# A third Strassen-Winograd step for three more quarter products, with VectorE's sums around the gates in another order

## The chip, the cores and the metric

The kernel runs on one core of one Trainium2 chip. The metric is the device time of one execution in microseconds, the median of several runs. Smaller is better.

## The reference, cut to what matters

`x` is 8 batches of 256 tokens of 1024 features, all in f32. Two layers with a residual follow each other. The first is a dense layer with a routed low-rank update: the router's logits get a bias for the batch's language id, the two best of 8 experts are softmax-weighted, and rank 4 factors `A` and `B` of these experts are added. The second is a dense layer whose 1024 x 1024 weight is picked for each batch by its adapter id.

```python
base   = einsum('btd,od->bto', x, W)
logits = einsum('btd,ed->bte', x, Wr) + one_hot(language_ids, 8)[:, None, :] * 5.0
topw, topi = top_k(logits, 2)
gates  = sum(one_hot(topi, 8) * softmax(topw)[..., None], axis=-2)
h      = einsum('btd,erd->bter', x, A)
x = x + base + 2.0 * einsum('bter,bte,eor->bto', h, gates, B)
x = x + einsum('bsi,boi->bso', x, weight[adapter_ids])
```

## The kernel before, in words

Features and tokens are split in two, so `x`, `W` and the result `y` are 2 x 2 blocks of 512 features by 1024 tokens (`xb`, `wb`, `yb`, in the on-chip memory all along). The residual is an identity added to the diagonal of the weights (`add_identity`). The first layer multiplies the blocks by the Strassen-Winograd scheme: seven products instead of eight, in the order 1, 5, 2, 6, 3, 7, 4, with sums of blocks ahead (`w_sum`, `x_sum`, in pieces of 1024 elements a partition) and sums of results behind (`join`). Each of the seven does the same once more inside: blocks are split in quarters, seven quarter products are made of sums `s1`..`s3` of weights and `t1`..`t3` of x, and `late` turns `s2` and `t2` into the fourth sums when the second quarter product has read them. A quarter product (`mm`) is four matmuls of 128 x 128 weights by 512 columns into a pair of accumulator banks. An f32 matmul is two instructions on TensorE.

In products 5, 2, 3 and 4 the quarter a(0,1) x b(1,0) goes a third step down: seven matmuls of 256 columns (`deep`, L513) instead of four of 512, with sums r1..r4 and q1..q4 of 128 and 256 elements. Three of the seven, P2 to P4, go straight into the accumulator X; P1, P6 and P7 are added up in one bank (`A3`) which is read between them, and P5 has its own (`B3`). Product 1 (`opening`), 6 and 7 have no third step. There are eight banks: three pairs (`pair0` to `pair2`), which play the roles A, X and B in turn (`roles`), and two single ones.

The router and low-rank part is `project(j, c)`: for half j of the tokens and half c of that, 32 matmuls of 136 columns that give h and the logits, chunk k of the features after chunk k. `take` adds the bias on VectorE and copies h on ScalarE. `gating(j)` is 18 small VectorE instructions, one exponential on ScalarE and a product of 1024 elements; `turn(j)` transposes the gated h on TensorE, whence `hg`, whose matmuls with `b_sb` and its differences (`bdiff`, made by `b_differences`) join the quarter products ("lora").

The order on each engine is the order of the code. Ahead of product 5 it is written out at the end of the code: project(1, 0), take, project(1, 1), take, gating(1) on VectorE beside project(0, 1) on TensorE, turn(1), product 5. x is replaced by a difference in place there (`t1(c, k)`, eight pieces of 512 elements).

From product 5 on, VectorE's work for later products stands in a list `todo` with a time and an earliest place for each item. `pump(place)` is called at seven places of each product and takes items in order until their time reaches an even share of what is left; place 7 takes all. The list before product 5 holds gating(0), the w_sum of w11 (two pieces, which product 6 needs) and make_subs("2"); before product 2 it holds x_sum of x12, w_sum of w21, make_subs("6") and two pieces of an x sum.

The second layer (`adapt`, L660) is one such scheme of seven products for each batch; the last batch is cut finer at the end (`adapt_last`, L718). Its weights come by `load_w1` on SP's queue, block by block, when the blocks whose place they take have been read.

Of the kernel before, what the change touches and what calls it, by code (L numbers as in the profile page):

```python
# [9 lines left out]
F32 = mybir.dt.float32  # L10
# [15 lines left out]
def kernel(  # L26
# [320 lines left out]
    def us(n):  # L347
        return (n + 151) / 960
# [13 lines left out]
        return pieces(fn, wb[out_], wb[x], wb[y], 2)  # L362

    subs = {}

    def make_subs(key, w, x, further=True):

        def a(i, j):  # L370
            return wb[w][:, 2 * j : 2 * j + 2, i * OQ : (i + 1) * OQ]

        def b(i, j):
            return xb[x][:, 2 * i : 2 * i + 2, j * TQ : (j + 1) * TQ]


        ra = lambda i, j: a(0, 1)[:, j, ts(i, P)]
        rb = lambda i, j: b(1, 0)[:, i, ts(j, TQ // 2)]
        t = {}

        def op3(name, tag, fn, x, y, first=4):
            width = P if name[0] == "r" else TQ // 2

            def run():
                t[name] = sub3.tile([P, width], F32, name=f"{name}_{key}", tag=tag)
                fn(t[name], *(t[v] if isinstance(v, str) else v for v in (x, y)))

            return us(width), first, run

        deep = [  # L390
            op3("r1", "r13", add, ra(1, 0), ra(1, 1)),
            op3("q1", "q13", minus, rb(0, 1), rb(0, 0)),
            op3("r2", "r2", minus, "r1", ra(0, 0)),
            op3("q2", "q2", minus, rb(1, 1), "q1"),
            op3("r4", "r4", minus, ra(0, 1), "r2"),
            op3("q4", "q4", minus, rb(1, 0), "q2"),
        ]

        def deep3():
            for o in (  # L400
                op3("r3", "r13", minus, ra(0, 0), ra(1, 0)),
                op3("q3", "q13", minus, rb(1, 1), rb(0, 1)),
            ):
                o[2]()

        def op(name, fn, x, y, first):
            pool = sub2 if name[1] == "2" else sub1
            width = OQ if name[0] == "s" else TQ

            def run():  # L410
                t[name] = pool.tile([P, 2, width], F32, name=f"{name}_{key}", tag=name)
                fn(t[name], *(t[v] if isinstance(v, str) else v for v in (x, y)))

            return us(2 * width), first, run

        def late_s():
            minus(t["s2"], a(0, 1), t["s2"])

        def late_t():
            minus(t["t2"], b(1, 0), t["t2"])  # L420

        subs[key] = (a, b, t, (late_s, late_t), (ra, rb, deep3), further)
        return [
            op("s1", add, a(1, 0), a(1, 1), 3),
            op("t1", minus, b(0, 1), b(0, 0), 3),
            op("s2", minus, "s1", a(0, 0), 3),
            op("t2", minus, b(1, 1), "t1", 3),
            op("s3", minus, a(0, 0), a(1, 0), 5),
            op("t3", minus, b(1, 1), b(0, 1), 5),
        ] + (deep if further else [])  # L430

    def evict(dest, acc, base=None):

        if base is None:
            nc.scalar.copy(dest, acc)  # L435
        else:
            add(dest, acc, base)
# [20 lines left out]
    def opening(key, dest):  # L458


        idle = pair("idle", 2)
        for i in range(WARM):
            nc.tensor.matmul(idle[:, 0, :P], lhsT=ident, rhs=ident, start=True, stop=True)  # L463
        mm = multiply()
        sums_of = make_subs(key, "11", "11", False)
        a, b, t, late, _, _ = subs.pop(key)
        X = pair(f"X_{key}", 0)
        A = pair(f"A_{key}", 1)
        add_identity(wb["11"], 0, 2)
        mm(X, a(0, 1), b(1, 0), True, part=(0,))  # L470
        project(0, 0, singles("ps_h_0_0"), (2,), last=False)
        mm(X, a(0, 1), b(1, 0), part=(1,))
        evict(dest[:, 0], X)
        project(0, 0, None, (3,), False, False)
        mm(A, a(0, 0), b(0, 0), True, part=(0,))
        project(0, 0, None, (0,), False, False)
        mm(A, a(0, 0), b(0, 0), part=(1,))
        project(0, 0, None, (1,), False, False)
        use_adapter_ids()
        add_identity(wb["11"], 2, 4)  # L480
        for s in sums_of[:4]:
            s[2]()
        add(dest[:, 0], A, dest[:, 0])
        nc.tensor.matmul(idle[:, 1, :NB], lhsT=ones, rhs=ids_f[:, :NB], start=True, stop=True)
        use_ids(idle[:, 1, :NB])
        B = pair(f"B_{key}", 2)
        mm(B, t["s1"], t["t1"], True)
        evict(dest[:, 3], B)
        for s in sums_of[4:]:
            s[2]()  # L490
        mm(A, t["s2"], t["t2"])
        evict(dest[:, 1], A)
        project(0, 0, None, range(KH, KC), False)
        take(0, 0)
        for f in late:
            f()
        mm(A, t["s3"], t["t3"])
        add(dest[:, 3], A, dest[:, 3])
        mm(B, t["s2"], b(1, 1))
        add(dest[:, 1], B, dest[:, 1])  # L500
        mm(A, a(1, 1), t["t2"])
        evict(dest[:, 2], A)

    def product(key, base, dest, lora=None, tokens=None):

        a, b, t, late, (ra, rb, deep3), further = subs.pop(key)
        mm = multiply(dict(zip("01d", b_part(lora))) if lora is not None else None, tokens)
        new = roles(key)
        old = [base[:, q] if base is not None else None for q in range(4)]
        n0, n1 = (slice(j * (TQ // 2), (j + 1) * (TQ // 2)) for j in range(2))  # L510

        def deep(acc, lhs, rhs, first=False):
            nc.tensor.matmul(acc, lhsT=lhs, rhs=rhs, start=first, stop=True, skip_group_check=True)  # L513

        def quarter(m, n):

            return dest[:, 0][:, m, n], old[0][:, m, n] if base is not None else None

        A = new("A")
        mm(A, a(0, 0), b(0, 0), True)  # L520
        X = new("X")
        nc.scalar.copy(X, A)
        if not further:
            pump(1)
            B = new("B")
            mm(B, t["s1"], t["t1"], True, "1", 1)
# [17 lines left out]
            evict(dest[:, 2], A, old[2])  # L544
            pump(7)
            return
        A3 = single(f"A3_{key}", 0)[:, n0]
        deep(A3, ra(0, 0), rb(0, 0), True)
        q, o = quarter(0, n0)
        evict(q, A3, o)  # L550
        pump(1)
        B = new("B")
        mm(B, t["s1"], t["t1"], True, "1", 1, ms=(0,))
        B3 = single(f"B3_{key}", 1)[:, n0]
        deep(B3, t["r1"], t["q1"], True)
        deep3()
        mm(A, t["s2"], t["t2"])
        evict(dest[:, 1], A, old[1])
        deep(A3, t["r2"], t["q2"])
        q, o = quarter(0, n1)  # L560
        evict(q, A3, o)
        late[0]()
        pump(2)
        mm(B, t["s1"], t["t1"], True, "1", 1, ms=(1,))
        evict(dest[:, 3], B, old[3])
        late[1]()
        pump(3)
        deep(X[:, 0, n0], ra(0, 1), rb(1, 0))
        deep(X[:, 0, n1], t["r4"], rb(1, 1))
        deep(X[:, 1, n0], ra(1, 1), t["q4"])  # L570
        mm(X, None, None, False, "0", 0, part=())
        deep(A3, t["r3"], t["q3"])
        two = [P, 2, TQ // 2]
        d1 = dest[:, 0][:, 1, :].rearrange("p (j n) -> p j n", j=2)
        both = A3.unsqueeze(1).to_broadcast(two)
        evict(d1, both, old[0][:, 1, :].rearrange("p (j n) -> p j n", j=2) if base is not None else None)
        add(dest[:, 0][:, :, n1], B3.unsqueeze(1).to_broadcast(two), dest[:, 0][:, :, n1])
        add(dest[:, 0], X, dest[:, 0])
        pump(4)
        mm(A, t["s3"], t["t3"])  # L580
        add(dest[:, 3], A, dest[:, 3])
        pump(5)
        mm(B, t["s2"], b(1, 1), False, "d", 1)
        add(dest[:, 1], B, dest[:, 1])
        pump(6)
        mm(A, a(1, 1), t["t2"], False, "1", 0)
        evict(dest[:, 2], A, old[2])
        pump(7)
# [169 lines left out]


    opening("1", y21)  # L760
    b_differences()
    add_identity(wb["22"])
    for t in w_sum(add, "21", "21", "22"):
        t[2]()
    subs5 = make_subs("5", "21", "12")
    subs5[0][2]()
    subs5[2][2]()
    project(1, 0, halves(pair("ps_h_1_0", 0)))
    take(1, 0)

    def t1(c, k):
        minus(xk(k, 1, c), xk(k, 1, c), xk(k, 0, c))

    for k in range(KH):
        t1(0, k)
    project(1, 1, halves(pair("ps_h_1_1", 2)))
    take(1, 1)
    for t in gating(1):
        t[2]()
    for k in range(KH):  # L780
        t1(1, k)
    project(0, 1, singles("ps_h_0_1"))
    turn(1, halves(pair("ps_g_1", 2)))
    take(0, 1)
    for i in (1, 6, 7, 3, 8, 9, 10, 11, 4, 5):
        subs5[i][2]()
    todo += gating(0)
    todo += w_sum(minus, "11", "21", "11")
    todo += make_subs("2", "12", "21")
    product("5", None, y22, 1, 1)  # L790
    turn(0, singles("ps_g_0"))
    todo += x_sum(minus, "12", "22", "12")
    todo += w_sum(minus, "21", "22", "11")
    todo += make_subs("6", "11", "12", False)
# [79 lines left out]
```

## Time and profile before

| what | us |
|---|---|
| median of 3 runs (429.12 to 429.49) | 429.25 |
| the profiled execution, with what lies around its span | 430.16 |
| span of the profiled execution | 428.4 |
| TensorE busy (PE) | 423.1 |
| VectorE busy (DVE) | 281.7 |
| ScalarE busy (ACT) | 39.6 |

Instructions are named by engine, line, tile written and tiles read. PE is the matmul side of TensorE, PEld its weight loads. A time in brackets with an arrow is the idle time of the engine just before the instruction, and what ended it. Matmuls are pipelined: a duration reaches into the next one, so that the pace is read from the distance of starts.

### The profile page before, as it was taken

What the parts mean: (1) busy time and instruction counts of PE and PEld (TensorE: products, weight loads), DVE (VectorE), ACT (ScalarE), POOL (GpSimd) and SP (SyncE); (2) the same over time, 40 slices, a digit from 0 to 9 for tenths busy, and PEclk for the clock granted to TensorE, in tenths of its full rate; (3) what the DMA queues carried; (4) which work ended last, traced back from release to release, by engine and by line L of the source; (5) the groups of instructions that cost most, each with busy time, mean ns of one, the idle gap of its engine ahead of it and who ended that gap; (6) DMA issues with size and microseconds to landing.
All of it is one profiled execution on the core that took longest, in us unless ns stands there. A gap on an engine that the chain in (4) does not pass through costs nothing.

```text
span 428.4 us, 3335 instructions
## 1 busy us (share of the span) xinstructions
PE 423.1 (99%) x1246; PEld 217.3 (51%) x1246; DVE 281.7 (66%) x375; ACT 39.6 (9%) x65; POOL 2.0 (0%) x10
## 2 busy tenths in 40 slices
PE   8999999999999999999999999999999999999996
PEld 5566984545444445444454444444444444444574
DVE  1627288956988959889595676565756576565531
ACT  1120022110000000000000101010110101010110
POOL 1000000000000000000000000000000000000000
PEclk9999999999999999999999999999999999999999
DMA  8995000000000140630302276556748385550202
GB/s 279 383 398 217 2 0 2 0 0 2 0 0 0 31 168 0 249 142 0 99 0 98 98 262 227 199 207 208 272 148 313 128 275 214 196 197 0 98 2 99
DMA packets 14305, 55.83 MB, mean 130 GB/s; under 512 B 1232, under 2 KB 3536, under 8 KB 9808
## 3 DMA queue, kind: packets, MB, share of 16 engines
q1 hardware_dynamic: 12976, 54.68, 35.5%
q10 hardware_dynamic: 1248, 0.93, 0.7%
q8 instruction: 10, 0.16, 0.2%
q14 instruction: 7, 0.06, 0.0%
q0 software_dynamic: 64, 0.00, 0.0%
HBM read 47.22 MB, written 8.39 MB: 130 GB/s over the span
## 4 chain that ended last, share of the span: by engine, by line
PE 98%; DVE 0%; POOL 0%; issue 0%; ACT 0%; POOLq 0%; DVEq 0%
PE A L447 24%; PE A L660 22%; PE B L447 14%; PE B L660 13%; PE ps_h L245 7%; PE X L660 6%; PE X L447 4%; PE A_last L718 3%; PE A L513 1%; PE X L513 1%; PE idle L463 1%; PE ps_g L315 0%; PE B L513 0%; DVE y L217 0%; ACT z L748 0%
## 5 line engine op out<-in xcount | busy, mean ns | idle before, releaser
L660 PE MATMUL B<-x,x 128*128 128x512 f32 x128 | 57.5, 592 | 0.0
L447 PE MATMUL A<-t,s 128*128 128x512 f32 x112 | 50.3, 592 | 0.0
L217 DVE TENSOR_TENSOR y<-A,y 128x1024 f32<-128x1024 f32 (+2 forms) x27 | 26.3, 985 | 25.1 <-PE A L447 14.2
L660 PE MATMUL A<-w,x 128*128 128x512 f32 x88 | 39.6, 592 | 0.0
L660 PEld LDWEIGHTS B<-x,x 128*128 128x128 f32 x128 | 24.3, 190 | 29.8 <-issue 29.7
L217 DVE TENSOR_TENSOR w<-w,w 128x1024 f32<-128x1024 f32 x24 | 29.0, 1223 | 15.4 <-PE A L660 15.3
L660 PE MATMUL A<-w,y 128*128 128x512 f32 x88 | 39.1, 592 | 0.0
L447 PEld LDWEIGHTS A<-t,s 128*128 128x128 f32 x112 | 21.2, 190 | 22.9 <-issue 22.5
L245 PEld LDWEIGHTS ps_h<-y,x 128*128 128x128 f32 x256 | 30.7, 191 | 3.3 <-issue 3.3
L245 PE MATMUL ps_h<-y,x 128*128 128x136 f32 x256 | 30.6, 279 | 0.0
L660 PEld LDWEIGHTS A<-w,x 128*128 128x128 f32 x88 | 16.7, 190 | 21.0 <-issue 21.0
L660 PEld LDWEIGHTS A<-w,y 128*128 128x128 f32 x88 | 16.7, 190 | 21.0 <-issue 21.0
L435 ACT COPY z<-A 128x512 f32<-128x512 f32 x21 | 12.3, 586 | 158.3 <-PE A L660 158.3
L447 PE MATMUL B<-t,s 128*128 128x512 f32 x56 | 25.9, 594 | 0.3 <-DVE bias L200 0.3
L447 PE MATMUL A<-x,w 128*128 128x512 f32 x56 | 25.3, 592 | 0.0
L447 PE MATMUL A<-t,w 128*128 128x512 f32 x56 | 25.2, 592 | 0.0
L447 PE MATMUL B<-x,s 128*128 128x512 f32 x56 | 25.2, 592 | 0.0
L217 DVE TENSOR_TENSOR y<-B,y 128x1024 f32<-128x1024 f32 (+1 forms) x16 | 17.4, 1090 | 9.5 <-PE B L447 8.7
L217 DVE TENSOR_TENSOR x<-x,x 128x1024 f32<-128x1024 f32 (+1 forms) x20 | 19.2, 1004 | 0.0
L447 PEld LDWEIGHTS B<-x,s 128*128 128x128 f32 x56 | 10.6, 190 | 13.4 <-issue 12.7
L447 PEld LDWEIGHTS A<-t,w 128*128 128x128 f32 x56 | 10.6, 190 | 13.4 <-issue 12.7
L217 DVE TENSOR_TENSOR z<-X,z 128x512 f32<-128x512 f32 x8 | 5.5, 692 | 17.9 <-PE X L660 15.9
(119 smaller groups left out, 446.3 us busy)
## 6 DMA issues: line engine op xcount, KB each, us to landing
x<-w_dram SPq DMA_DIRECT2D x24, 1024.0 KB, 4.8
w<-w_dram SPq DMA_DIRECT2D x8, 1024.0 KB, 4.8
out_dram<-z SPq DMA_DIRECT2D x15, 512.0 KB, 3.0
x<-xT_dram SPq DMA_DIRECT2D x6, 1024.0 KB, 12.9
w<-wT_dram SPq DMA_DIRECT2D x3, 1024.0 KB, 14.9
x<-xT_dram SPq DMA_DIRECT2D x4, 256.0 KB, 3.8
x<-xT_dram SPq DMA_DIRECT2D x2, 512.0 KB, 7.4
w<-w11T_dram SPq DMA_DIRECT2D x1, 512.0 KB, 6.1
```

Source lines behind the costliest of these rows:

```text
L217: nc.vector.tensor_tensor(out_, x, y, op)
L245: nc.tensor.matmul(ps[v][:, u * EA : (u + 1) * EA], lhsT=xk(k, j, c)[:, ts(r, P)], rhs=aw_sb[:, k, :], start=(first and k == some[0] and u ...
L435: nc.scalar.copy(dest, acc)
L447: nc.tensor.matmul(acc[:, m, :], lhsT=l, rhs=r, start=(first and i < len(ms)), stop=(i >= len(steps) - len(ms)), skip_group_check=True,)
L463: nc.tensor.matmul(idle[:, 0, :P], lhsT=ident, rhs=ident, start=True, stop=True)
L513: nc.tensor.matmul(acc, lhsT=lhs, rhs=rhs, start=first, stop=True, skip_group_check=True)
L660: nc.tensor.matmul(accs[name], lhsT=lhs[:, k // 2, k % 2, :], rhs=rhs[:, k, :], start=(first and k == 0), stop=(k == KH - 1), skip_group_c ...
L718: nc.tensor.matmul(acc, lhsT=lhs[:, k // 2, k % 2, :], rhs=rhs[:, k, ts(v, m)], start=(first and k == 0), stop=(k == KH - 1), skip_group_c ...
```

## The change

A function `third` makes the sums and pieces of a third step for any quarter product: `ops` are r1 to q4, `ops3` r3 and q3, `piece(n)` is the matmul Pn, and `take(n, ...)` adds or copies the accumulated bank into the part of the result that it belongs to. Three more quarters use it: in product 1 the quarters with s2 x b(1,1) and a(1,1) x t2 (P3 and P4 of the quarter products), and in product 4 the one with a(1,1) x t2 (P4).

In product 1 the eight chunks of project(1, 0) are moved between the pieces, and b_differences with them. VectorE's x sums (now `x_t1`), s1 and s2 of product 5 are put in the order of their use: two x sums ahead of the gates, the other six and s1, s2 behind them. The ids' product goes into pair 0. The w_sum of w11 is put on the list after product 5, ahead of product 2's work.

```diff
+    def third(key, lhs, rhs):
...
+        ops = [
+            op("r1", "r13", add, A(1, 0), A(1, 1)),
+            op("q1", "q13", minus, B(0, 1), B(0, 0)),
+            op("r2", "r2", minus, "r1", A(0, 0)),
+            op("q2", "q2", minus, B(1, 1), "q1"),
+            op("r4", "r4", minus, A(0, 1), "r2"),
+            op("q4", "q4", minus, B(1, 0), "q2"),
+        ]
+        def ops3():
+            op("r3", "r13", minus, A(0, 0), A(1, 0))[2]()
+            op("q3", "q13", minus, B(1, 1), B(0, 1))[2]()
+        def piece(n, acc=None):
+            if n in (1, 5):
+                own[n] = single(f"P{n}_{key}", n // 5)[:, n0]
+            out_, l, r = {
+                1: lambda: (own[1], ra(0, 0), rb(0, 0)),
+                2: lambda: (acc[:, 0, n0], ra(0, 1), rb(1, 0)),
+                3: lambda: (acc[:, 0, n1], t["r4"], rb(1, 1)),
+                4: lambda: (acc[:, 1, n0], ra(1, 1), t["q4"]),
+                5: lambda: (own[5], t["r1"], t["q1"]),
+                6: lambda: (own[1], t["r2"], t["q2"]),
+                7: lambda: (own[1], t["r3"], t["q3"]),
+            }[n]()
+            nc.tensor.matmul(out_, lhsT=l, rhs=r, start=(n in (1, 5)), stop=True, skip_group_check=True)
...
 # opening
-        nc.tensor.matmul(idle[:, 1, :NB], lhsT=ones, rhs=ids_f[:, :NB], start=True, stop=True)
-        use_ids(idle[:, 1, :NB])
+        wide = pair("ids_wide", 0)[:, 0, :NB]
+        nc.tensor.matmul(wide, lhsT=ones, rhs=ids_f[:, :NB], start=True, stop=True)
+        use_ids(wide)
...
-        for f in late:
-            f()
+        late[0]()
+        ops, ops3, piece, out = third(f"{key}b", lambda: t["s2"], lambda: b(1, 1))
+        for o in ops:
+            o[2]()
+        late[1]()
         mm(A, t["s3"], t["t3"])
         add(dest[:, 3], A, dest[:, 3])
-        mm(B, t["s2"], b(1, 1))
+        quarter = halves(pair("ps_h_1_0", 0))
+        chunk = lambda k: project(1, 0, quarter, (k,), k == 0, k == KC - 1)
+        chunk(0)
+        piece(1)
+        out(1, dest[:, 1], dest[:, 1])
+        piece(5)
+        ops3()
+        chunk(1)
+        piece(6)
+        out(6, dest[:, 1], dest[:, 1])
+        chunk(2)
+        b_differences()
+        for n in (2, 3, 4):
+            piece(n, B)
+        chunk(3)
+        piece(7)
+        out(7, dest[:, 1], dest[:, 1])
+        last_out = out
+        ops, ops3, piece, out = third(f"{key}a", lambda: a(1, 1), lambda: t["t2"])
+        for o in ops[:2]:
+            o[2]()
+        last_out(5, dest[:, 1], dest[:, 1])
+        for o in ops[2:]:
+            o[2]()
         add(dest[:, 1], B, dest[:, 1])
-        mm(A, a(1, 1), t["t2"])
-        evict(dest[:, 2], A)
+        chunk(4)
+        piece(1)
+        out(1, dest[:, 2])
+        chunk(5)
+        piece(5)
+        ops3()
+        chunk(6)
+        piece(6)
+        out(6, dest[:, 2])
+        for n in (2, 3, 4):
+            piece(n, A)
+        chunk(7)
+        piece(7)
+        out(7, dest[:, 2])
+        out(5, dest[:, 2], dest[:, 2])
+        add(dest[:, 2], A, dest[:, 2])
...
 # product, for key 4 (two): after P5 of the first third step
+        if two:
+            ops, ops3, piece, take = third(f"{key}b", lambda: a(1, 1), lambda: t["t2"])
+            for o in ops:
+                o[2]()
...
         add(dest[:, 3], A, dest[:, 3])
+        if two:
+            piece(1)
+            take(1, dest[:, 2], old[2])
         pump(5)
         mm(B, t["s2"], b(1, 1), False, "d", 1)
+        if two:
+            piece(5)
+            ops3()
+            piece(6)
+            take(6, dest[:, 2], old[2])
         add(dest[:, 1], B, dest[:, 1])
         pump(6)
+        if two:
+            mm(A, None, None, False, "1", 0, part=())
+            for n in (2, 3, 4):
+                piece(n, A)
+            piece(7)
+            take(7, dest[:, 2], old[2])
+            take(5, dest[:, 2], dest[:, 2])
+            add(dest[:, 2], A, dest[:, 2])
+            pump(7)
+            return
...
 # around the gates
     opening("1", y21)
-    b_differences()
     add_identity(wb["22"])
     for t in w_sum(add, "21", "21", "22"):
         t[2]()
...
     take(1, 0)
+    x_t1(0, 0)
+    x_t1(0, 1)
     project(1, 1, halves(pair("ps_h_1_1", 2)))
     take(1, 1)
+    run(*(g[2] for g in gating(1)))
     project(0, 1, singles("ps_h_0_1"))
     turn(1, halves(pair("ps_g_1", 2)))
+    x_t1(1, 0)
+    x_t1(1, 1)
+    s1()
+    t1()
     take(0, 1)
+    x_t1(0, 2)
+    x_t1(0, 3)
+    run(r1, q1, s2)
+    x_t1(1, 2)
+    x_t1(1, 3)
+    run(t2, r2, q2, r4, q4, s3, t3)
     todo += gating(0)
-    todo += w_sum(minus, "11", "21", "11")
     todo += make_subs("2", "12", "21")
     product("5", None, y22, 1, 1)
     turn(0, singles("ps_g_0"))
+    todo += w_sum(minus, "11", "21", "11")
     todo += x_sum(minus, "12", "22", "12")
```

More of the change, by code (lines that the diff above doesn't have):

```diff
@@ L364, with op, run, take @@
     subs = {}
+    NQ = TQ // 2
+    def third(key, lhs, rhs):
+        ra = lambda i, j: lhs()[:, j, ts(i, P)]
+        rb = lambda i, j: rhs()[:, i, ts(j, NQ)]
+        n0, n1 = slice(0, NQ), slice(NQ, TQ)
+        t, own = {}, {}
+        def op(name, tag, fn, x, y):
+            width = P if name[0] == "r" else NQ
+            def run():
+                t[name] = sub3.tile([P, width], F32, name=f"{name}_{key}", tag=tag)
+                fn(t[name], *(t[v] if isinstance(v, str) else v() for v in (x, y)))
+            return us(width), 4, run
+        A, B = (lambda i, j: lambda: ra(i, j)), (lambda i, j: lambda: rb(i, j))
+        ops = [
[22 more added lines that the diff above has]
+            nc.tensor.matmul(out_, lhsT=l, rhs=r, start=(n in (1, 5)), stop=True, skip_group_check=True)
+        def take(n, dest, base=None):
+            cut = lambda v: {1: v[:, 0, n0], 6: v[:, 0, n1], 5: v[:, :, n1]}[n]
+            if n == 7:
+                cut = lambda v: v[:, 1, :].rearrange("p (j n) -> p j n", j=2)
+            src = own[5 if n == 5 else 1]
+            if n in (5, 7):
+                src = src.unsqueeze(1).to_broadcast([P, 2, NQ])
+            evict(cut(dest), src, None if base is None else cut(base))
+        return ops, ops3, piece, take
     def make_subs(key, w, x, further=True):
@@ L374, in b @@
             return xb[x][:, 2 * i : 2 * i + 2, j * TQ : (j + 1) * TQ]
-        ra = lambda i, j: a(0, 1)[:, j, ts(i, P)]
-        rb = lambda i, j: b(1, 0)[:, i, ts(j, TQ // 2)]
         t = {}
[L381 to L404, printed above, removed]
         def op(name, fn, x, y, first):
@@ L420, in late_t @@
             minus(t["t2"], b(1, 0), t["t2"])
-        subs[key] = (a, b, t, (late_s, late_t), (ra, rb, deep3), further)
+        deep = third(key, lambda: a(0, 1), lambda: b(1, 0)) if further else None
+        subs[key] = (a, b, t, (late_s, late_t), deep)
         return [
@@ L429, in make_subs @@
             op("t3", minus, b(1, 1), b(0, 1), 5),
-        ] + (deep if further else [])
+        ] + (deep[0] if further else [])
     def evict(dest, acc, base=None):
@@ L465, in opening @@
         sums_of = make_subs(key, "11", "11", False)
-        a, b, t, late, _, _ = subs.pop(key)
+        a, b, t, late, _ = subs.pop(key)
         X = pair(f"X_{key}", 0)
@@ L494, in opening @@
         take(0, 0)
-        for f in late:
-            f()
+        late[0]()
[3 more added lines that the diff above has]
+        late[1]()
         mm(A, t["s3"], t["t3"])
         add(dest[:, 3], A, dest[:, 3])
-        mm(B, t["s2"], b(1, 1))
-        add(dest[:, 1], B, dest[:, 1])
-        mm(A, a(1, 1), t["t2"])
-        evict(dest[:, 2], A)
+        quarter = halves(pair("ps_h_1_0", 0))
[22 more added lines that the diff above has]
+            o[2]()
+        add(dest[:, 1], B, dest[:, 1])
+        chunk(4)
[14 more added lines that the diff above has]
+        add(dest[:, 2], A, dest[:, 2])
     def product(key, base, dest, lora=None, tokens=None):
-        a, b, t, late, (ra, rb, deep3), further = subs.pop(key)
+        a, b, t, late, deep = subs.pop(key)
         mm = multiply(dict(zip("01d", b_part(lora))) if lora is not None else None, tokens)
@@ L509, in product @@
         old = [base[:, q] if base is not None else None for q in range(4)]
[L510 to L517, printed above, removed]
         A = new("A")
@@ L522, in product @@
         nc.scalar.copy(X, A)
-        if not further:
+        if deep is None:
             pump(1)
@@ L546, in product @@
             return
[L547 to L550, printed above, removed]
+        two = key == "4"
+        _, ops3, piece, take = deep
+        piece(1)
+        take(1, dest[:, 0], old[0])
         pump(1)
@@ L553, in product @@
         mm(B, t["s1"], t["t1"], True, "1", 1, ms=(0,))
-        B3 = single(f"B3_{key}", 1)[:, n0]
-        deep(B3, t["r1"], t["q1"], True)
-        deep3()
+        piece(5)
+        ops3()
         mm(A, t["s2"], t["t2"])
         evict(dest[:, 1], A, old[1])
-        deep(A3, t["r2"], t["q2"])
-        q, o = quarter(0, n1)
-        evict(q, A3, o)
+        piece(6)
+        take(6, dest[:, 0], old[0])
         late[0]()
@@ L567, in product @@
         pump(3)
-        deep(X[:, 0, n0], ra(0, 1), rb(1, 0))
-        deep(X[:, 0, n1], t["r4"], rb(1, 1))
-        deep(X[:, 1, n0], ra(1, 1), t["q4"])
+        for n in (2, 3, 4):
+            piece(n, X)
         mm(X, None, None, False, "0", 0, part=())
[L572 to L577, printed above, removed]
+        piece(7)
+        take(7, dest[:, 0], old[0])
+        take(5, dest[:, 0], dest[:, 0])
+        if two:
+            ops, ops3, piece, take = third(f"{key}b", lambda: a(1, 1), lambda: t["t2"])
+            for o in ops:
+                o[2]()
         add(dest[:, 0], X, dest[:, 0])
@@ L581, in product @@
         add(dest[:, 3], A, dest[:, 3])
+        if two:
+            piece(1)
+            take(1, dest[:, 2], old[2])
         pump(5)
         mm(B, t["s2"], b(1, 1), False, "d", 1)
+        if two:
+            piece(5)
+            ops3()
+            piece(6)
+            take(6, dest[:, 2], old[2])
         add(dest[:, 1], B, dest[:, 1])
         pump(6)
+        if two:
+            mm(A, None, None, False, "1", 0, part=())
+            for n in (2, 3, 4):
+                piece(n, A)
+            piece(7)
+            take(7, dest[:, 2], old[2])
[3 more added lines that the diff above has]
+            return
         mm(A, a(1, 1), t["t2"], False, "1", 0)
@@ L764, with x_t1, run @@
         t[2]()
[L765 to L768, printed above, removed]
+    subs5 = [t[2] for t in make_subs("5", "21", "12")]
+    s1, t1, s2, t2, s3, t3, r1, q1, r2, q2, r4, q4 = subs5
+    def x_t1(c, k):
+        minus(xk(k, 1, c), xk(k, 1, c), xk(k, 0, c))
+    def run(*fns):
+        for f in fns:
+            f()
     take(1, 0)
[L771 to L775, printed above, removed]
+    x_t1(0, 0)
+    x_t1(0, 1)
     project(1, 1, halves(pair("ps_h_1_1", 2)))
     take(1, 1)
[L778 to L781, printed above, removed]
+    run(*(g[2] for g in gating(1)))
     project(0, 1, singles("ps_h_0_1"))
     turn(1, halves(pair("ps_g_1", 2)))
+    x_t1(1, 0)
+    x_t1(1, 1)
+    s1()
+    t1()
     take(0, 1)
-    for i in (1, 6, 7, 3, 8, 9, 10, 11, 4, 5):
-        subs5[i][2]()
+    x_t1(0, 2)
[4 more added lines that the diff above has]
+    run(t2, r2, q2, r4, q4, s3, t3)
     todo += gating(0)
-    todo += w_sum(minus, "11", "21", "11")
     todo += make_subs("2", "12", "21")
```

## The prediction

> **What bounds the kernel now.** First the page's busy shares and the chain that ended last, then the waits, then the timeline at the places the change touches.
>
> ```profile
> PE 423.1 (99%) x1246; PEld 217.3 (51%) x1246; DVE 281.7 (66%) x375; ACT 39.6 (9%) x65; POOL 2.0 (0%) x10
> PE 98%; DVE 0%; POOL 0%; issue 0%; ACT 0%; POOLq 0%; DVEq 0%
> ```
>
> The chain of waits is TensorE for 98% of the span, so one microsecond of TensorE work removed is one microsecond of time, unless a new wait takes its place. VectorE has a third of the span free, but not everywhere: the windows view gives it 5.87 us busy of 7.13 between 53.37 and 60.5, and 28.15 of 31.5 in the first product after the gates.
>
> The waits view filtered to PE holds two rows, the warm-up and this:
>
> ```profile
> PE B L447 <- DVE bias L200: 0.3, 1, 0.3
> ```
>
> ```profile
> 16.67 0.38 PE L484 MATMUL idle<-ids_f,ones 1*128 1x8 f32 x2
> 17.09 0.23 DVE L200 TENSOR_TENSOR bias<-idle,ecol 128x64 f32<-128x64 f32 x1
> 17.36 0.30 PEld L447 LDWEIGHTS B<-t,s 128*128 128x128 f32 x2 [0.41 <-DVE bias L200]
> 17.37 3.70 PE L447 MATMUL B<-t,s 128*128 128x512 f32 x8 [0.32 <-DVE bias L200]
> 20.90 0.59 PE L447 MATMUL A<-t,s 128*128 128x512 f32 x1
> ```
>
> The bank pair of the ids' product is also B's, so B waits until VectorE has read it (17.32). After this point the chain in order of time holds only TensorE to the end. Two of its rows give the prices (an f32 matmul is two instructions; a row's mean duration overlaps the next, so distances between starts count):
>
> ```profile
> 28.21 3.43 PE A L447 x8
> 65.06 0.43 PE A L513 x2
> ```
>
> Eight instructions of 512 columns take 3.43 us, 0.429 each; two of 256 columns 0.43, 0.215 each, exactly half, with no gap before or behind.
>
> **What the Trainium skill says.** "TensorE: Matmul & The Clock Gate", section "Step-by-step: what each phase is for", says that only weight loads are pulled ahead, matmuls stay in order. The trace agrees: the weight load above waits 0.41, and everything behind it on TensorE waits with it. "VectorE: DVE Perf Modes", section "The TRN2 errata", prices an f32 tensor_tensor at (N+151)/0.96 ns: 291, 424, 691 and 1224 ns for 128, 256, 512 and 1024 elements. The rows here show 288, 420, 686 and 1221. Back to back they start about 0.085 us closer than that (four of 512 take 2.49 us in all), and 0.03 later than the end if they need the one just before.
>
> **Part 1, three quarters a third step down.** A quarter product is four matmuls of 512 columns, 8 x 0.429 = 3.43 us. In seven pieces of 256 columns it is 14 x 0.2145 = 3.00. So 0.43 saved, three times: **-1.29 us**. The 56 such instructions of L513 in the trace show no idle time before them, which bounds the doubt to a few hundredths a piece. Projection chunks between the pieces are moved, not added (8 x 0.116 = 0.93 each, as in the opening already).
>
> **Part 2, ids' product in pair 0.** Pair 0 was last read by ScalarE's copy of X (10.56 to 11.57), so nothing waits there; its next user is chunk 0, 14 us later. Without the wait B can start one short matmul after the second half of L484 (16.80), at about 16.93, and A at 20.37 instead of 20.90 (B's 17.37 to 20.90 is 3.53, so a restart costs 0.10 above 3.43). **-0.52 us**; at least the 0.3 of the waits row.
>
> **Part 3, new waits.** I walked all three queues in program order with these durations, 0.04 us for a hand-over (DVE's 256-element add starts 0.04 behind its matmul's end at 96.85), the shift of part 2 included. On the old order the walk puts the transposes at 60.54 (trace: 60.58) and the next product at 92.75 (92.82).
>
> *End of the opening.* P1, P6 and P7 of one quarter share a bank, so each needs the reading of the one before. One chunk (0.93) covers a hand-over of 0.16 (matmul tail) + 0.04 + 0.42 + 0.04 = 0.66 if VectorE is free. VectorE reads out(1) from 32.54 to 32.96; P6 is due at 33.67: covered by 0.7. P7's reading is 512 elements, 0.69, hence 0.93 against chunk 4's 0.93: the next P1 is due at 38.60 and the bank is free at 38.60, too late to load its weights ahead. **+0.10** (bounds 0 and 0.2). b_differences (1.6 us) lies in VectorE's idle time before P7.
>
> *Gates.* Behind P7 of the second quarter VectorE has ScalarE's copy to wait for (to 45.3), then 0.69 + 1.22 + 0.69 + 2.36 of sums, two takes with ScalarE between them (0.8) and two x sums (1.3): free at 52.2, where project(1, 1) ended at 52.1. So the gates start 0.1 late. They took 53.37 to 59.94 = 6.57, so end at 58.8; project(0, 1) (64 x 0.116 = 7.42) leaves the transposes due at 59.3. Covered by 0.5, as now (59.94 to 60.47).
>
> *The first product behind the gates.* Its x sums, s1 and s2 were before the gates and now lie behind. From 58.75: six x sums of 0.60, s1 and s2 of 0.60 each, t1 1.14, takes 0.17, r1 0.20, q1 0.34, and t2 0.12 + 1.22 bring t2's end to 66.75. TensorE needs it at 59.3 + 0.88 (transposes) + 3.43 + 0.43 + 2.58 + 0.43 = 67.05. Covered by 0.3, the thinnest cover of all; cost 0 (bounds 0 and 0.7, the latter with ScalarE between the takes and 0.05 more per hand-over).
>
> *Product 2.* w11's two pieces of w_sum move from product 5 into it. Its list of work grows from 15.5 to 17.9 us, 2.56 a place instead of 2.22. The two pieces of w21 thereby slide to place 4, where s1 and t1 stood: 2 x 1.135 instead of 0.60 + 1.135, 0.53 more before the add that frees A. That add has no room today:
>
> ```profile
> 116.60 1.22 DVE L217 TENSOR_TENSOR y<-A,y 128x1024 f32<-128x1024 f32 x1
> 117.87 0.48 PEld L447 LDWEIGHTS A<-t,w 128*128 128x128 f32 x2 [0.38 <-DVE y L217]
> 118.16 1.02 PE L447 MATMUL A<-t,w 128*128 128x512 f32 x2
> ```
>
> The weight load already waits for it and the matmul just makes its slot (117.73 + 0.43). With 0.53 more the add ends at 118.35, the matmul starts at 118.40, 0.24 late, plus 0.10 for the restart: **+0.34 us** (bounds 0.1 and 0.5). Later VectorE idles over 2 us in product 6, which ends it.
>
> *Product 4.* VectorE gets six sums (2.0), r3 and q3 (0.54), and four evictions (about 2.1) for one of 1.22. It idles 2.3 before the add of B (227.41) and 2.6 before the last eviction (232.56). The walk finds each piece's input ready over 0.2 early, and the two y sums for the adapter's second and third matmul over 3 us early; A is read 0.6 before its bank is rewritten. Cost 0; if that cover is gone, 0.2. DMA queues: no issue on SP, ACT or POOL changes place; SP's transfers for the adapter wait on the same readers. project(1, 0) reads x from 31 us on instead of 38; its first x block is the third of six transfers issued from 7.1 to 18.8 us, at a median of 12.9 to landing: an estimate of 25 us.
>
> **Sum.** -1.29 - 0.52 + 0.10 + 0.34 = **-1.37 us**. The profiled execution had a span of 428.4 and 430.16 with what lies around it, 0.91 above the median of the runs (429.25). The difference holds for either: 428.8 for an execution like that one, **427.9** for the median.
>
> **Rivals.**
> 1. *The moved sums are late*: t2 behind the gates stops TensorE. For: 0.3 of cover, on a chain of some thirty VectorE instructions with two exchanges with ScalarE. Against: the same chain today keeps its 0.5. At 0.7 the time is 428.6, a gain of 0.7, within what a measurement of this kernel can tell (about 0.2%, 0.86 us).
> 2. *No new waits*: VectorE is a little quicker than walked and product 2's add costs nothing: -1.81, 427.4. Against: the weight load at 117.87.
> 3. *Slower: VectorE becomes the bound from the opening to the gates.* Between 27.7 and 59 it gets 16 third-step sums and eight adds that wait for pieces or products; if each of these exchanges costs VectorE 0.4 more than walked (the takes' exchange with ScalarE costs 0.44), they make 3.2 us. The place where it would show is the transposes: beyond 0.5 us of lateness every microsecond is TensorE's. It turns the gain into a loss of over 0.86 from 0.5 + 1.37 + 0.86 = 2.7 us of lateness on; at 3.2 us, 429.25 - 1.37 + 2.7 = 430.6. Against: VectorE waits nearly 3 us for P7 of the second quarter at 42.4 to 45.3 in the walk, which absorbs all lateness before it.
> 4. *The change doesn't do what it says*: the pieces run no shorter than the quarters, since each needs its own fresh weights. Then 428.3 with part 2 and no new waits, 428.7 with them. The L513 rows speak against it.
>
> **How the numbers follow.** Forecast with its small variants 0.56, rival 1 0.17, rival 2 0.14, rival 3 0.09, rival 4 0.04. Low end: all waits gone, 427.3. High end: rival 1 with product 2's wait at its bound, 428.9; rival 3 is left out. Faster by over 0.2%: forecast nearly whole (0.54), rival 2, half of 1 (its cost spreads from 0.3 to 0.7, and 0.5 is the border): 0.77. Within 0.2%: the rest of 1 and 4, some of 3: 0.15. Slower by over 0.2%: 0.08.
>
> **What would show it.** B starts at about 16.95 and no row "PE B <- DVE bias" is left; three times 14 piece instructions at 0.215 stand where eight of 0.43 stood; the transposes start about 1.2 us earlier than 60.58; the first waits of PE in the new list are A of product 2 behind VectorE's add of y (0.2 to 0.3) and perhaps P1 of the second quarter. Wrong it is if PE's waits list t2 behind the gates or the transposes (rivals 1 and 3), or if the pieces stand further apart than 0.215.

## The result, and the profile after

| | before | after |
|---|---|---|
| median of 9 runs, us | 429.12 | 428.22 |
| ratio of the times (95% interval) | | 0.9971 (0.9963 to 0.9980) |
| span of the profiled execution, us | 428.4 | 426.2 |

By the ratio with its interval, the change makes the kernel faster by 0.29%, 1.2 us (0.9 to 1.6). The two medians lie only 0.90 apart, and the nine runs of either kernel spread over 1.4 us. The forecast was 427.9, a gain of 1.37; the median came out 0.3 above it.

The page's busy shares and the chain that ended last, by engine:

```profile
PE 421.2 (99%) x1264; PEld 220.4 (52%) x1264; DVE 293.4 (69%) x409; ACT 40.0 (9%) x67; POOL 2.0 (0%) x10
PE 95%; DVE 3%; issue 0%; POOL 0%; ACT 0%; POOLq 0%; DVEq 0%
```

TensorE has 18 instructions more (3 x 6) and is busy 1.9 us less; VectorE has 34 more and is busy 11.7 us more. The chain has VectorE in it now: in order of time it runs through VectorE from 101.22 to 116.25, up to the place in product 2 that is shown below. The waits view filtered to PE has lost its row for the ids' product, and only the warm-up (the kernel's first matmuls, on an identity) is left:

```profile
PE idle L495 <- POOL ident masks.py:199: 1.4, 1, 1.4
```

**The two spans can't be subtracted as they stand.** The ids' product, the first instruction that the change touches, starts at 16.67 us before and at 15.64 after, though the code ahead of it is the same. Over the twelve profiles of this study that start lies anywhere from 14.96 to 16.67. The difference between these two arises in the first four instructions of 512 columns, up to about 7 us. Before, the weight loads there take 0.34 us each and start 0.86 apart (5.26, 6.12, 6.97), twice the later distance; after, the slow pace ends behind the load at 5.32, and the next ones, at 5.83 and 6.26, take 0.19 and start 0.43 apart. The waits for incoming data that the trace names there are 0.20 and 0.26 us, so they are not the difference; what ends the slow pace is open. So 1.03 of the 2.2 us between the spans is start-up. I therefore count D, the time from the start of the ids' product to the end of the last matmul. D comes from one execution of each kernel, but it repeats well: in the four profiles whose code is the same up to the transposes (the change and three of the experiments), these start at 42.83 in all four.

| counted from the start of the ids' product, us | before | after | difference | so far forecast |
|---|---|---|---|---|
| B of product 1 starts | 0.70 | 0.32 | -0.38 | -0.44 |
| the next A starts | 4.23 | 3.85 | -0.38 | -0.52 |
| transposes behind the gates | 43.91 | 42.83 | -1.08 | -1.28 |
| transposes behind product 5 | 75.28 | 74.19 | -1.09 | -1.28 |
| first product of the second layer | 215.68 | 214.53 | -1.15 | -1.37 |
| D, end of the last matmul | 408.20 | 407.05 | -1.15 | -1.37 |

The timeline at the ids' product, in answer to the lines shown of before:

```profile
15.64 0.38 PE L517 MATMUL ids_wide<-ids_f,ones 1*128 1x8 f32 x2
15.95 0.30 PEld L479 LDWEIGHTS B<-t,s 128*128 128x128 f32 x2
15.96 3.70 PE L479 MATMUL B<-t,s 128*128 128x512 f32 x8
16.06 0.23 DVE L200 TENSOR_TENSOR bias<-ids_wide,ecol 128x64 f32<-128x64 f32 x1
...
19.49 0.59 PE L479 MATMUL A<-t,s 128*128 128x512 f32 x1
```

B starts 0.32 behind the ids' product, ahead of VectorE's reading at 16.06. But its first eight instructions still take 19.49 - 15.96 = 3.53, with no wait in front of them.

The chain in order of time at the end of product 4, first before, where twelve A instructions stood together, eight of the quarter and four of the low-rank part, and then after:

```profile
227.37 5.15 PE A L447 x12
232.52 2.58 PE A L660 x6
```

```profile
226.03 0.86 PE P_4b L411 x4
226.89 1.72 PE A L479 x4
228.61 1.30 PE A L411 x6
229.91 0.43 PE P_4b L411 x2
230.34 1.72 PE A L741 x4
```

With P1 earlier (0.43) the fourteen piece instructions take 0.43 + 0.86 + 1.30 + 0.43 = 3.02 where eight took 3.43. The four A instructions of L479 between them are the low-rank part.

The timeline in product 2, in answer to the lines of before at 116.60:

```profile
112.75 2.35 DVE L217 TENSOR_TENSOR w<-w,w 128x1024 f32<-128x1024 f32 x2
...
115.02 1.22 DVE L217 TENSOR_TENSOR y<-A,y 128x1024 f32<-128x1024 f32 x1
...
116.29 0.30 PEld L479 LDWEIGHTS A<-t,w 128*128 128x128 f32 x2 [0.90 <-DVE y L217]
116.29 3.70 PE L479 MATMUL A<-t,w 128*128 128x512 f32 x8
```

The two w pieces now stand in front of the add, and the weight load waits 0.90 where it waited 0.38. The matmul starts with its weight load instead of 0.29 behind it. It was due at 114.33 + 4 x 0.429 = 116.05: 0.24 late. (The prediction looked for this wait in the waits view for PE, which lists no row for it: the preceding matmul's recorded end, 114.33 + 1.88 = 116.21, reaches over most of the gap. It is the weight load's row that tells.)

### The profile page after: what moved, and what is told of

It is laid out like the page before. It is cut to its first block, busy times and chain, and to the rows that moved or that the text cites. A ratio compares the mean times of both kernels' runs of the same rounds, so it can differ in the third digit from the quotient of the medians.

```text
span 426.2 us, 3410 instructions
## 1 busy us (share of the span) xinstructions
PE 421.2 (99%) x1264; PEld 220.4 (52%) x1264; DVE 293.4 (69%) x409; ACT 40.0 (9%) x67; POOL 2.0 (0%) x10
## 4 chain that ended last, share of the span: by engine, by line
PE 95%; DVE 3%; issue 0%; POOL 0%; ACT 0%; POOLq 0%; DVEq 0%
PE A L741 23%; PE A L479 22%; PE B L741 13%; PE B L479 12%; PE ps_h L245 7%; PE X L741 6%; PE X L479 4%; PE A_last L799 3%; PE P L411 1%; DVE y L217 1%; DVE x L217 1%; PE X L411 1%; PE idle L495 1%; PE A L411 1%; DVE w L217 1%; PE P_1a L411 0%
## 5 line engine op out<-in xcount | busy, mean ns | idle before, releaser
L479 PE MATMUL A<-t,s 128*128 128x512 f32 x112 | 50.3, 592 | 0.0
L245 PEld LDWEIGHTS ps_h<-y,x 128*128 128x128 f32 x256 | 31.7, 190 | 3.3 <-issue 2.9
L479 PEld LDWEIGHTS A<-t,s 128*128 128x128 f32 x112 | 21.2, 190 | 22.9 <-issue 22.5
L245 PE MATMUL ps_h<-y,x 128*128 128x136 f32 x256 | 31.9, 279 | 0.0
L217 DVE TENSOR_TENSOR y<-A,y 128x1024 f32<-128x1024 f32 x19 | 23.2, 1221 | 11.5 <-PE A L479 11.3
L479 PE MATMUL B<-t,s 128*128 128x512 f32 x56 | 25.9, 594 | 0.0
L479 PE MATMUL A<-x,w 128*128 128x512 f32 x56 | 25.3, 592 | 0.0
L479 PE MATMUL B<-x,s 128*128 128x512 f32 x48 | 21.6, 592 | 0.0
L479 PE MATMUL A<-t,w 128*128 128x512 f32 x40 | 18.1, 595 | 0.1
L217 DVE TENSOR_TENSOR y<-B,y 128x1024 f32<-128x1024 f32 x12 | 14.6, 1219 | 5.1 <-PE B L479 5.1
L217 DVE TENSOR_TENSOR t<-x 128x1024 f32<-128x1024 f32 x14 | 17.0, 1217 | 0.3 <-DMA x<-xT_dram 0.3
L217 DVE TENSOR_TENSOR t<-x,t 128x1024 f32<-128x1024 f32 x14 | 17.0, 1217 | 0.0
```

What stands on the lines that cost most here:

```text
L217: nc.vector.tensor_tensor(out_, x, y, op)
L245: nc.tensor.matmul(ps[v][:, u * EA : (u + 1) * EA], lhsT=xk(k, j, c)[:, ts(r, P)], rhs=aw_sb[:, k, :], start=(first and k == some[0] and u ...
L479: nc.tensor.matmul(acc[:, m, :], lhsT=l, rhs=r, start=(first and i < len(ms)), stop=(i >= len(steps) - len(ms)), skip_group_check=True,)
```

## The experiments

Each edit is made to the changed kernel unless said otherwise. D is 408.20 before and 407.05 after the change.

**w11's w_sum back on product 5's list.**

```diff
+    todo += w_sum(minus, "11", "21", "11")
     todo += make_subs("2", "12", "21")
     product("5", None, y22, 1, 1)
     turn(0, singles("ps_g_0"))
-    todo += w_sum(minus, "11", "21", "11")
```

> The changed kernel with the w_sum of w11 back on VectorE's list ahead of product 5. Measured as D, the time from the start of the ids' product to the end of the last matmul, which leaves out the start-up (408.2 us before, 407.1 after the change). My theory (the moved w_sum delays the add that frees A in product 2): the weight load of A<-t,w waits for VectorE no longer beyond its slot, D falls by 0.34 to 406.7, and nothing new waits in product 5. Rival (product 5 is the tighter place now that its sums lie behind the gates): product 5 gets a wait of 0.2 or more, D stays at 407.1 or rises.

Measured: D 406.71, ratio to before 0.9968 (0.9956 to 0.9980). The same place in its timeline:

```profile
115.26 1.22 DVE L217 TENSOR_TENSOR y<-A,y 128x1024 f32<-128x1024 f32 x1
...
116.53 0.48 PEld L479 LDWEIGHTS A<-t,w 128*128 128x128 f32 x2 [0.37 <-DVE y L217]
116.82 3.60 PE L479 MATMUL A<-t,w 128*128 128x512 f32 x8
```

The 0.34 is back, the lines look as before the change, and the transposes behind product 5 stand at 74.20 as with the change (74.19). Product 5 had the room; putting this sum on the later list cost 0.34.

**The ids' product in B's pair again.**

```diff
-        wide = pair("ids_wide", 0)[:, 0, :NB]
+        wide = idle[:, 1, :NB]
```

> The changed kernel with the ids' product in the bank pair of B again. Theory A (the wait itself is all that the other bank saves): D rises by 0.38 to 407.4, the difference of the starts of B in the two traces; B's first eight instructions take 3.53 us with and without the wait. Theory B (as predicted, the wait and 0.10 for a restart): D rises by 0.52 to 407.6.

Measured: D 407.43, that is +0.38; ratio 0.9975 (0.9967 to 0.9983). B starts at +0.70 and its first eight instructions take 3.54 us with the wait, 3.53 without. This is theory A: what the forecast took for the price of a restart is there in both cases.

**Product 4 without its new third step.**

```diff
-        two = key == "4"
+        two = False
```

> The changed kernel with P4 of product 4 as four matmuls of 512 columns again. Theory (14 x 0.2145 against 8 x 0.429, all of VectorE's extra work covered): D rises by 0.43 to 407.5. Rival (VectorE's eleven extra instructions cost something in the first batch of the second layer): D rises by less than 0.3.

Measured: D 407.47, +0.42; ratio 0.9980 (0.9973 to 0.9988). VectorE's additional work in product 4 is covered whole.

**The opening without its third steps.** Both quarters as four matmuls again, with project(1, 0) behind them.

```diff
...
         late[1]()
         mm(A, t["s3"], t["t3"])
         add(dest[:, 3], A, dest[:, 3])
+        mm(B, t["s2"], b(1, 1))
+        add(dest[:, 1], B, dest[:, 1])
+        mm(A, a(1, 1), t["t2"])
+        evict(dest[:, 2], A)
+        b_differences()
+        quarter = halves(pair("ps_h_1_0", 0))
+        project(1, 0, quarter)
-        chunk = lambda k: project(1, 0, quarter, (k,), k == 0, k == KC - 1)
-        chunk(0)
-        piece(1)
...
```

> The changed kernel with both quarters of the opening as four matmuls of 512 columns again and project(1, 0) in one behind them; ids' bank, VectorE's order around the gates, the w_sum of w11 and product 4 as changed. Theory (two quarters at 0.43 less 0.12 for the wait of P1): D rises by 0.74 to 407.8, with the transposes 0.74 later against the ids' product. Rival (the pieces cost something between the chunks, or VectorE's work in the opening delays the gates): D rises by less than 0.5 or not at all.

Measured: D 407.75, +0.70, all of it at the transposes (+43.53 against +42.83); ratio to before 0.9990 (0.9980 to 1.0000). Two third steps at 0.43 less 0.12 make 0.74; 0.04 stays unaccounted for.

**VectorE's sums in the old order.**

```diff
+    run(s1, s2)
     take(1, 0)
-    x_t1(0, 0)
-    x_t1(0, 1)
+    for k in range(KH):
+        x_t1(0, k)
...
     run(*(g[2] for g in gating(1)))
+    for k in range(KH):
+        x_t1(1, k)
...
```

> The changed kernel with VectorE's sums around the gates in the old order: s1, s2 and all four x sums of the first quarter ahead of the gates, the other four straight behind them. Theory (VectorE has no idle time left between the opening and the gates, and the cover behind the gates is 0.5): s1, s2 and two x sums put 0.6 x 4 + 0.1 = 2.5 us ahead of the gates, the transposes start 2.0 later against the ids' product and D rises by 2.0 to 409.1, slower than before the change by 0.9. Rival (the order matters little, since the sums are VectorE's work on either side): D rises by less than 0.5, and t2's wait goes away.

Measured: D 409.27, +2.2; ratio to before 1.0061 (1.0037 to 1.0085). The time is slower than before the change. Its timeline at the transposes:

```profile
59.02 1.22 DVE L217 TENSOR_TENSOR y<-y,y 128x1024 f32<-128x1024 f32 x1
60.16 2.49 DVE L217 TENSOR_TENSOR x<-x,x 128x512 f32<-128x512 f32 x4
...
60.38 1.06 PE L315 MATMUL ps_g<-ident,y 128*128 128x128 f32 x8 [2.03 <-DVE y L217]
```

The last product of the gates (59.02 + 1.22 = 60.24) releases the transposes, which stood idle for 2.03 us. The transposes come 2.19 later in all; the 0.16 beyond the recorded wait are what the recorded end of the matmul before them reaches past its pace (the projection's matmuls: 0.28 recorded, 0.116 from start to start).

**Neither the opening's third steps nor the new order.** To the kernel with the opening undone, the old order as in the last diff.

> The kernel of the opening's quarters undone, with VectorE's sums around the gates in the old order as well. Theory (the new order of the sums gains nothing by itself; it makes the room that the pieces of the opening take from VectorE ahead of the gates): without the pieces the gates' cover is there in the old order too, no wait appears, and D stays at 407.75. Rival (the order of use is worth something by itself): D rises by 0.3 or more.

Measured: D 407.75, no wait, the transposes at +43.53; ratio to before 0.9996 (0.9985 to 1.0007), where a D shorter by 0.45 (0.1%) would give 0.9990, within the interval. The same D with either order, to the hundredth: the order of use is worth nothing by itself, and 2.2 us as soon as the opening's third steps take VectorE's time ahead of the gates.

**More VectorE work ahead of the gates.**

```diff
     x_t1(0, 1)
+    b_differences()
     project(1, 1, halves(pair("ps_h_1_1", 2)))
```

> The changed kernel with b_differences made a second time on VectorE (1.65 us, the same values) between the second x sum and the takes ahead of gating(1). Theory (VectorE is free just as project(1, 1) ends, and the transposes' cover is 0.50): the gates start 1.6 later, the transposes wait 1.1 and D rises by 1.1 to 408.2; t2 behind them gets no wait. Rival (VectorE has more room there than the walk shows): D rises by less than 0.5. Rival (no cover at all): D rises by 1.6.

Measured in one execution: D 408.45, +1.40. From its waits view:

```profile
PE ps_g L315 <- DVE y L217: 1.0, 1, 1.0
```

Counted from the ids' product, the last gate product ended 1.63 later and the transposes started 1.16 later, so 0.47 was covered (cover: how long an input is ready before it is needed). Another 0.25 arose in product 5, where I had expected none: t2 ends at 67.04, and the weight load of A, which needs s2 and t2, starts just behind it, at 67.16. The profile names no releaser there; that t2 is the cause is read from the order.

**More VectorE work in the opening**, where the forecast's slower rival sat.

```diff
         out(6, dest[:, 2])
+        b_differences()
         for n in (2, 3, 4):
             piece(n, A)
```

> The changed kernel with b_differences made a second time on VectorE (1.65 us, the same values) in the opening, behind r3 and q3 of the second quarter, where VectorE waits 2.9 us for P7 and ScalarE's copy. Theory (that idle time takes up all lateness of the opening, so the opening's many small exchanges can't reach the gates): D stays at 407.1, the transposes at +42.8 behind the ids' product. Rival (the prediction's slower case: VectorE is the bound from the opening to the gates, and every microsecond more shows at the transposes): D rises by 1.1 to 1.6.

Measured in one execution: the transposes at +42.83 to the hundredth, D 407.22, +0.17. The idle time before the copy's add shrank from 2.90 to 1.30 as meant:

```profile
45.13 0.69 DVE L217 TENSOR_TENSOR y<-P_1a,y 128x512 f32<-128x512 f32 x1 [1.30 <-ACT y L467]
46.34 1.23 DVE L217 TENSOR_TENSOR y<-A,y 128x1024 f32<-128x1024 f32 x1 [0.52 <-DVE y L217]
```

But the second add came 1.21 behind the first, where with the change alone it was 0.80 (44.46 and 45.26). These 0.41 were still covered at the transposes (0.50), but t2 ended 0.41 later as well, and the 0.17 arose in product 5, between the transposes and +74.36, where the change has +74.19. In the eight other profiles with these two adds they start 0.79 or 0.80 apart; why the second was late in this one execution is open.

**Product 3 as well.**

```diff
-        two = key == "4"
+        two = key in ("3", "4")
```

> The changed kernel with P4 of product 3 a third step down as well, by the same code as in product 4. TensorE's part is -0.43 again. Theory (VectorE's room decides, not the arithmetic: its list in product 3 leaves it idle 1.4 us before the last eviction, and it gets 4.5 us more): the add that frees A at the end of product 3 is late, B of product 7 waits 1.2 for it and 0.1 for its weight load, and D rises by 0.9 to 407.9. Rival (each further third step is worth 0.43 as long as VectorE is below 75% busy): D falls by 0.4 to 406.6.

Measured: D 407.96, +0.91; ratio to before 1.0000 (0.9992 to 1.0009): in the runs' times the gain of the whole change is gone; by D 0.24 of it is left. From its timeline, at the start of product 7:

```profile
177.68 1.41 DVE L217 TENSOR_TENSOR y<-P_3b,y 128x512 f32<-128x512 f32 x2
...
179.12 1.22 DVE L217 TENSOR_TENSOR y<-A,y 128x1024 f32<-128x1024 f32 x1
...
180.38 1.22 DVE L217 TENSOR_TENSOR y<-y,y 128x1024 f32<-128x1024 f32 x1
...
180.50 3.67 PE L479 MATMUL B<-t,s 128*128 128x512 f32 x8 [1.08 <-DVE y L217]
```

The add of A ends at 180.34 and B of product 7, which gets A's pair, starts at 180.50 with 1.08 us of waiting. The pieces themselves were as short as elsewhere (0.43 for two instructions, 174.10 to 175.82).

**Both of the change's own waits taken out.** w11 as in the first experiment, and:

```diff
         chunk(4)
+        chunk(5)
         piece(1)
         out(1, dest[:, 2])
-        chunk(5)
         piece(5)
```

> The changed kernel with w11's w_sum on the list of product 5, and chunk 5 of project(1, 0) moved ahead of P1 of the opening's second quarter, so that two chunks (1.86 us) instead of one lie between P7 of the first quarter and P1, which needs its bank. Theory (P1 stands 0.53 behind the chunk instead of 0.43 because the bank comes free only as it is due): D falls by another 0.12 from the 406.7 without product 2's wait to 406.6, and P5 and P6 find their sums and banks ready. Rival (P5 or P6, now with one chunk less behind P1, waits for VectorE's last reading of P5 of the first quarter or for q1): D stays at 406.7 or rises. In time it should beat the kernel before by 1.6 us, a ratio of 0.9963.

Measured: D 406.58; ratio to before 0.9965 (0.9952 to 0.9977), 1.5 us. The timeline of the changed kernel at P1 of the second quarter, and then of this one:

```profile
36.99 0.69 DVE L217 TENSOR_TENSOR y<-P_1b,y 128x512 f32<-128x512 f32 x1 [1.55 <-PE P_1b L411]
...
37.74 0.30 PEld L411 LDWEIGHTS P_1a<-t,w 128*128 128x128 f32 x2
37.74 0.70 PE L411 MATMUL P_1a<-t,w 128*128 128x256 f32 x2
```

```profile
36.66 0.69 DVE L217 TENSOR_TENSOR y<-P_1b,y 128x512 f32<-128x512 f32 x1 [1.55 <-PE P_1b L411]
...
38.20 0.30 PEld L411 LDWEIGHTS P_1a<-t,w 128*128 128x128 f32 x2
38.31 0.59 PE L411 MATMUL P_1a<-t,w 128*128 128x256 f32 x2
```

In the changed kernel the weights are loaded at 37.74, when the bank has just come free (36.99 + 0.69 = 37.68), and the matmul has no lead of its weight load. With two chunks in between, the load comes 0.11 ahead, and the wait is gone: the transposes stand at +42.70, 0.13 earlier. This version is the fastest by D: 1.62 shorter than before, 0.47 shorter than the change. In the medians (428.04 against 428.22) the two can't be told apart; D tells them.

## Why the prediction was right, step by step

- **What bounds the kernel**: right. Each piece of TensorE's time that went or came showed at the end of the last matmul, to within 0.05 in every experiment that added no wait.
- **Part 1, -1.29**: product 4 gave 0.41 (0.42 when undone), the opening's two gave 0.70 net of P1's wait, against 0.76 forecast. In the opening the chain gives 3.01 for the first quarter's pieces and 3.13 for the second's, with 0.55 instead of 0.43 at that P1. Rival 4 is out. (Its times were also added up wrongly: with nothing from part 1, -0.52 leaves 428.7 without new waits and 429.2 with them, not 428.3 and 428.7. The ends of the stated range lie about 0.15 beyond what their terms give, 427.4 and 428.7.)
- **Part 2, -0.52**: the term that was mis-sized; it measured -0.38. The failed step is "a restart costs 0.10 above 3.43", applied to B: the 3.53 stay without the wait. B's start was also 0.06 too early in the forecast (+0.26; it came at +0.32). In the trace B's first weight load and first matmul start together (15.95 and 15.96) without the wait too, whereas further on the load leads (A's first load at 19.07, its first matmul at 19.49). That the two short matmuls of the ids' product leave no time for a load to run ahead fits this and was not tested. At the two places where the bank or VectorE really held the stream up, the 0.10 is about right: 0.34 less 0.24 in product 2, and 0.12 to 0.13 at P1.
- **End of the opening, +0.10 at P1**: 0.12 in the chain, 0.13 by taking it out. P6's bank was in time, as walked.
- **Gates**: cover 0.5 forecast; in the trace the last gate product ends at 57.86 and the transposes' weights load at 58.36. The experiments with the old order and with more work ahead agree: the last gate product ended 2.66 and 1.63 us later and the transposes started 2.19 and 1.16 later, so 0.47 was covered both times.
- **t2 behind the gates, cost 0**: right for the change (t2 ends at 65.76, 0.24 ahead of its weight load at 66.00 and 0.46 ahead of its matmul, which starts on time at 66.22; 0.3 was walked). Its being the thinnest cover was borne out: with more VectorE work ahead of the gates and in the opening, t2 ended 0.47 and 0.41 later against the transposes, and product 5 lost 0.25 and 0.17. So only about 0.24 of the distance could be used, that to the weight load. Rival 1 was the right place and did not happen.
- **Product 2, +0.34**: 0.34 by taking it out. The Trainium skill, "TensorE: Matmul & The Clock Gate", section "Step-by-step: what each phase is for", says that weight loads are pulled ahead of matmuls in flight. The trace agrees: before the change this load, though it had waited 0.38, started 0.29 ahead of its matmul (117.87 and 118.16), so the wait cost nothing. Those 0.29 were all the room there was; the 0.53 of forecast lateness left 0.24.
- **Rival 3, slower**: its place was wrong. Lateness in the opening is taken up by the wait for P7, as the prediction argued against it: with 1.65 us more work there the transposes stayed at +42.83. A slower kernel was near all the same, by another way: without the new order of sums the changed kernel is 0.6% slower than before.

The sum forecast was -1.37 and D says -1.15. Of the 0.22 between, 0.14 is part 2 and the rest is spread over the opening and product 4 in pieces of 0.02 to 0.06.

## What to carry to other kernels

When an engine is busy for 99% of the span, price an edit by the distance of its instructions' starts, and spend the effort on walking the other engines' queues: here the same third step gained 0.4 us in product 4 and lost 0.9 in product 3, where VectorE had no room before one add. Look for weight loads that already wait, at no cost: here that was the place where half a microsecond of lateness cost 0.34. And when start-up spreads by more than the change is worth, count from the first instruction that the change touches.

## What the runs showed of the hardware

- Start-up: the same code ahead of the ids' product took from 14.96 to 16.67 us in twelve profiled executions, a spread of 1.7 us, more than the change brings. In the profile of before the first weight loads stand 0.86 us apart up to the one at 6.97, in that of after 0.43 apart from 5.83 on.
- Two VectorE adds, 512 and then 1024 elements, into the same part of the result started 0.79 or 0.80 us apart in eight profiles and 1.21 apart in one, with four VectorE instructions more ahead of them. There the trace lists 0.52 of waiting and names only the add before as its end.
